# First sequence's chain, the mixer's beginning and the attention's last denominators: a change of order on one Trainium2 core

## The chip, the cores and the metric

The kernel runs on one core of one Trainium2 chip. The metric is the device time of one execution in microseconds (us), the median of several executions. The core has five engines with instruction queues of their own: PE (TensorE: matmuls and transposes, with its weight loads shown apart as PEld), DVE (VectorE), ACT (ScalarE: activation functions, whose tables are loaded by an instruction of its own), POOL (GpSimd) and SP (SyncE, which here issues the DMAs). Each runs its queue in order and waits at an instruction until the semaphores that it needs are set.

## The reference, cut to what matters

The input `x` is 8 sequences of 1024 tokens (32 × 32) with 128 channels, fp32. Two layers:

```python
x = x + attention(_gn(x))          # group norm, 4 heads of 32
t = _to_tokens(x)
t = t + mixer(_ln_t(t))            # two directions
t = t + spectral(_ln_t(t))         # filters by FFT, one of four banks chosen
```
Attention projects q, k and v, divides q and k by their lengths over the tokens, takes `softmax(10 * q k^T)` (in the kernel: Exp of the scores, their sums as denominators, reciprocals), multiplies with v and with `w_out`, and adds a bias. The mixer is, for each direction, an input projection, a causal convolution of four taps with SiLU, a step size `dt = softplus(x + bias)`, and a chunked state-space sum:

```python
Acs = jnp.cumsum(dAc, axis=2)
Lmat = jnp.exp(_segsum(dAc.transpose(0, 1, 3, 2)))
Y_diag = jnp.einsum('bcln,bcsn,bchls,bcshp->bclhp', Cc, Bc, Lmat, xc)
decay_st = jnp.exp(Acs[:, :, -1:, :] - Acs)
states = jnp.einsum('bcln,bclh,bclhp->bchpn', Bc, decay_st, xc)
new = st + carry * dec[:, :, None, None]     # from chunk to chunk
Y_off = jnp.einsum('bcln,bchpn,bclh->bclhp', Cc, prev, jnp.exp(Acs))
y = Y_diag + Y_off + xh * D
yn = rmsnorm(y * silu(z)) @ out_proj
```
Chunks are 64 tokens long, with 4 heads. The spectral stage needs, besides, tables of sines and a weight bank chosen by a softmax over four numbers.

## The kernel before, in words

The program is one launch in four stages: attention (0 to about 449 us), mixer (to about 1010), spectral stage with the filter matrices (to about 1370), and the end. Within attention the order of PE, DVE, ACT and POOL is the order of the program text; SP's is not fixed. Within the mixer all five are in the order of the text. So the Python text is the schedule: generators that `yield` are pieces of work that a loop picks up, one piece per slot.

**Start.** Sequence 0 is normalised and projected by the same generator as the others, `qkv` (L607), with `first` switching some steps: PE turns the tokens (`xt`, L612), ACT copies them, DVE takes statistics (L623), PE sums them over groups (`pm` L628, `pv` L636), POOL takes the root (`gn`), DVE scales (`xnt`, L641). PE projects `pq` and `pk` (L648); DVE copies each out of PSUM (L656), ACT squares each with a running sum (`junk`, L660), POOL makes the lengths (L665, L667), PE projects `pvl` (L671), DVE scales k (L684). Between these, lines 774–785 place the pieces of `transforms` (L311), which makes angle tables on POOL and DVE (`angles`, L282) for two trigonometric tables, `inv` and `fwd`, and for four lag tables; `sines` (L300) turns angles to sines on ACT.

**Attention.** 128 units: 8 sequences × 2 halves of queries × 8 key tiles. In slot n of the loop, `scores` (L692) issues unit n's matmuls (`pt`) and Exp (`pr`), `weigh` (L715) weighs v by unit n−1's (`po`), `total` (L738) sums denominators (`pd`) of two key tiles at a time. At the end of a half, `weighted` (L751) copies the denominators, takes four reciprocals in two pieces, the largest and the smallest of them (`most`, `least`), multiplies `av`, and `project` (L425) multiplies by `w_out` (`py`) and adds to X. The slots also take pieces of the next sequence's `qkv`, of `mixer_and_bank` (weights of the mixer, then `select_bank`, L205, then the mixing of the bank's matrices on POOL), of `transforms`, of the filters' taps, and, at the end, the first sequence's `dt` (`steps`, L480: bias, `sp_e` = Exp, `sp_u` = 1 + e, `sp_l` = Ln, `dt`, `da`).

**Mixer.** 16 units: 8 sequences × 2 directions (u.d 0 and 1). Lines 1253–1274 prepare the first unit by hand: `project_x` and `copy_x` for two halves (`pp`, `xp`), `add_decays` (L870: cumulative sums, `pdec`, copied to `cums` and `dsum` on ACT), what is left of `weighted` for the last half of attention with its projection `last_py`, `first_tap` (L970, ACT) and `convolve` (L976, DVE) for the taps, `turn_decays` (L885), `take_decays` (L891: Exp of `cums`, one store to DRAM and four loads that spread it over partitions, into `lm` and `ec`), `from_row` (L920, POOL, on `lm`), `project_bc` and `activate_bc` (`pb`, then `bt` and `ct`), and `compare_denominators` (L431: a test of the denominators' range, `far`, `pf`). `wide_psum(ps_w)` and `wide_psum(ps_s)` hand out slots of two PSUM pools.

The loop L1277–1352 then takes one unit `u` per turn and prepares the one `following`: `between` (L930, ACT, Relu then Exp on `lm`), `turn_x` (`sx`), `weigh_start` (POOL, `ec`), `turn_b` (`sb`, `bg`), the following unit's projections (`pp`), `weigh_decays`, the previous unit's `end` (L1239), `steps` for the next sequence where one is `fresh` (in turns with u.d = 0: 0, 2, …, 12), `project_z` and `activate_z` (`pz`, `zs`), `from_row(following)`, `chunk_states` and `pass_states` (`pst`, `state`, `moved`), the last tap, `project_bc`, and `outputs` in two halves (`sy`).

## Time and profile before

| | us |
|---|---|
| time, median of 3 executions (1420.01 to 1421.38) | 1420.11 |
| the profiled execution | 1414.25 |
| its span in the trace | 1412.4 |
| PE busy in it | 1325.0 |
| DVE busy | 1093.9 |
| ACT busy | 916.0 |
| POOL busy | 530.2 |
| mean granted TensorE clock, of full speed | 0.987 |

The profile is of one execution. A row of the timeline has its start from the span's beginning, its duration (of a run of like instructions together, with their number after x), the engine, the line, the operation, output and inputs by their names in the program, and, in brackets, how long the engine had been idle before it and what ended that idleness. A row of the waits has what waited, for what, the sum, the number and the longest. Matmuls are pipelined, and weight loads lie beside them. The busy share of a stage tells which engine bounds it, and only a wait on that engine, or at a place where it idles, costs time.

Times of the stages' ends that are used: attention's last product starts at 447.46, the mixer's first projection at 451.20, its first turn at 471.91 (`sx`), and the next turns' `sx` at 501.94, 534.37 and 569.40.

### The profile page before, as it was taken

How to read it: one execution, taken by the hardware profiler on the slowest of the kernel's cores; microseconds unless marked ns; L12 is line 12 of the kernel's file. 1: busy time of each engine (PE TensorE's matmuls, PEld its weight loads, DVE VectorE, ACT ScalarE, POOL GpSimd, SP SyncE). 2: the span in 40 equal slices, each digit the busy share in tenths (PEclk: the TensorE clock that was granted, in tenths of full speed). 3: DMA queues.
4: the chain of work that ended last, by engine and by line, in shares of the span. 5: the costliest groups of instructions: out<-in, count | busy, mean ns of one | idle time of the engine just before them, and what ended most of it. 6: DMA issues, size and time to landing. Idle time of an engine off the chain costs nothing. (4 is left out here: it accounts for less than half of the span.)

```text
span 1412.4 us, 45313 instructions
## 1 busy us (share of the span) xinstructions
PE 1325.0 (94%) x19798; PEld 836.2 (59%) x19798; DVE 1093.9 (77%) x2141; ACT 916.0 (65%) x1423; POOL 530.2 (38%) x510
## 2 busy tenths in 40 slices
PE   5999999999999899999999999998799899999977
PEld 2323333233333466666666666665689899999964
DVE  6789888787768698978897988889644677777745
ACT  3766666766757777878787878786454555555530
POOL 2426865875610333425243434343476111111100
PEclk9999999999999999999999999999999999999999
DMA  7101111110000543434344445441459233222257
GB/s 179 46 1 31 46 38 38 38 50 27 8 1 2 124 86 77 107 77 106 82 102 91 104 92 114 89 110 42 135 189 233 76 86 81 72 78 71 71 186 299
DMA packets 139382, 123.09 MB, mean 87 GB/s; under 512 B 44808, under 2 KB 118152, under 8 KB 135080
## 3 DMA queue, kind: packets, MB, share of 16 engines
q1 hardware_dynamic: 137048, 115.93, 32.1%
q10 hardware_dynamic: 2128, 4.19, 0.8%
q8 instruction: 157, 2.57, 0.8%
q14 instruction: 49, 0.40, 0.1%
HBM read 78.15 MB, written 34.08 MB: 79 GB/s over the span
## 5 line engine op out<-in xcount | busy, mean ns | idle before, releaser
L707 ACT ACTIVATE pr<-pt 128x1024 f32<-128x1024 f32 x256 | 248.1, 1021 | 114.9 <-PE pt L702 113.5
L732 DVE TENSOR_TENSOR two<-pr,pr 128x1024 f32<-128x1024 f32 x128 | 162.3, 1308 | 19.2 <-ACT pr L707 18.7
L1525 ACT COPY gs<-pg 128x512 f32<-128x512 f32 x256 | 132.4, 603 | 64.1 <-PE pg L1512 48.3
L1523 DVE COPY gs<-pg 128x512 f32<-128x512 f32 x256 | 158.7, 683 | 14.7 <-PE pg L1512 9.7
L702 PE MATMUL pt<-q,k 32*128 32x512 f32 x1024 | 157.6, 648 | 9.4 <-ACT pr L707 4.7
L1512 PE MATMUL pg<-taps,mst 32*128 32x128 f32 x4096 | 145.6, 281 | 4.2 <-ACT gs L1525 3.4
L1512 PEld LDWEIGHTS pg<-taps,mst 32*128 32x128 f32 x4096 | 133.8, 190 | 16.2 <-issue 11.4
L723 PE MATMUL po<-pr,v 128*32 128x512 f32 x1024 | 139.7, 603 | 0.0
L938 POOL TENSOR_TENSOR ec<-ec,ct 128x2048 f32<-128x2048 f32 x16 | 83.6, 5226 | 131.8 <-ACT cums L880 69.8
L1546 PE MATMUL py<-gs,u 128*32 128x128 f32 (+1 forms) x4096 | 128.5, 277 | 1.2 <-issue 1.2
L1002 PE MATMUL pb<-bxt,wbc 128*128 128x512 f32 x256 | 115.7, 605 | 11.0 <-ACT zs L993 11.0
L980 DVE SCALAR_TENSOR_TENSOR xs<-xp,cw,xs 128x1024 f32<-128x1024 f32 x96 | 121.7, 1281 | 1.7
L1546 PEld LDWEIGHTS py<-gs,u 128*32 128x32 f32 (+1 forms) x4096 | 112.4, 141 | 8.7 <-issue 1.5
L1535 POOL TENSOR_SCALAR u<-u 128x512 f32<-128x512 f32 x16 | 23.9, 1495 | 227.8 <-DMA u<-ud 114.0
L702 PEld LDWEIGHTS pt<-q,k 32*128 32x128 f32 x1024 | 46.6, 185 | 87.2 <-issue 33.1
L1002 PEld LDWEIGHTS pb<-bxt,wbc 128*128 128x128 f32 x256 | 47.7, 191 | 69.3 <-issue 54.9
L1099 DVE SCALAR_TENSOR_TENSOR state<-state,dec,pst 128x64 f32<-128x64 f32 x448 | 87.3, 274 | 1.5 <-DVE state L1096 0.5
L1208 POOL TENSOR_TENSOR rms<-rms_v,mhalf 128x8 f32<-128x8 f32 x16 | 27.1, 1696 | 159.7 <-DVE rms_v L1206 159.7
L723 PEld LDWEIGHTS po<-pr,v 128*32 128x32 f32 x1024 | 27.6, 110 | 88.3 <-issue 84.1
L924 POOL TENSOR_TENSOR lm<-cs,lm 128x2048 f32<-128x2048 f32 x16 | 57.9, 3620 | 46.9 <-DVE xs L980 31.4
L743 PE MATMUL pd<-two,ones 128*32 128x512 f32 x512 | 73.9, 612 | 0.2
L1178 PEld LDWEIGHTS spo<-wo,y 128*128 128x128 f32 x512 | 62.2, 192 | 15.3 <-issue 10.2
(288 smaller groups left out, 2757.7 us busy)
## 6 DMA issues: line engine op xcount, KB each, us to landing
lm<-cd SPq DMA_DIRECT2D x32, 512.0 KB
ec<-cd SPq DMA_DIRECT2D x32, 512.0 KB
ud<-sp SPq DMA_DIRECT2D x8, 1024.0 KB
u<-ud SPq DMA_DIRECT2D x32, 256.0 KB
yd<-sums SPq DMA_DIRECT2D x32, 256.0 KB
moved<-state SPq DMA_DIRECT2D x48, 128.0 KB
room<-yd SPq DMA_DIRECT2D x6, 1024.0 KB
X<-in_x SPq DMA_DIRECT2D x8, 512.0 KB
```

Source lines behind the costliest of these rows:

```text
L702: nc.tensor.matmul(pt[:, i, :], lhsT=k[rows, j * P : (j + 1) * P], rhs=q[rows, cols], start=True, stop=True)
L707: nc.scalar.activation(pr[:, 2 * g : 2 * g + 2, :].rearrange("p i t -> p (i t)"), pt.rearrange("p i t -> p (i t)"), AF.Exp, scale=SCALE,)
L723: nc.tensor.matmul(po[rows, :], lhsT=vs[b][:, j, rows], rhs=pr[:, h, :], start=(j == 0), stop=(j == NT - 1))
L732: nc.vector.tensor_tensor(two, sums["pr"][:, 2 * g : 2 * g + 2, :], pr[:, 2 * g : 2 * g + 2, :], ALU.add)
L938: t = nc.gpsimd.tensor_tensor(u.ec, u.ec, u.ct.unsqueeze(1).to_broadcast([P, NH, NT, L]), ALU.mult)
L980: u.convolved = nc.vector.scalar_tensor_tensor(acc, xp[:, at : at + T], cw[u.d][:, n, i : i + 1], acc, ALU.mult, ALU.add)
L1002: nc.tensor.matmul(u.pb[:, i * 512 : (i + 1) * 512], lhsT=wbc[u.d][:, k, :], rhs=xt[:, at : at + 512], start=(k == 0), stop=(k == KC - 1),)
L1099: nc.vector.scalar_tensor_tensor(u.state[:, k, h, :], u.state[:, k - 1, h, :], u.dec[:, c, h, j : j + 1], u.pst[c][:, j, h, :], ALU.mult, ...
L1512: nc.tensor.matmul(pts[g][:, e, :], lhsT=mst[rows, n * 4 + e, :], rhs=taps[rows, cols].rearrange("p f q m i -> p (f q m i)"), start=True, ...
L1523: nc.vector.tensor_copy(to, frm)
L1525: nc.scalar.copy(to, frm)
L1546: nc.tensor.matmul(py[t * 32 : t * 32 + 32 - 16 * m, q // 2, :], lhsT=u[:, i, m:, :, :, q * FC + f].rearrange("p k b i -> p (k b i)"), rhs ...
```

## The change

It has these parts:

- **First sequence**: a function of its own, `first_qkv`, takes the place of `qkv(0)`. DVE's statistics and ACT's copy take opposite halves of the turned tokens; 24 transposes whose result nobody reads (`busy`) are put on PE in three places; a Sin of one column (`soon`) loads the Sin table; the squares read PSUM; k is scaled out of PSUM; `fwd`'s and `inv`'s sines are taken there; the bias is added after k. `transforms` makes `fwd`'s angles first, then `inv`'s. The Sin of `fwd` leaves the later burst with the lag tables.
- **Bank choice**: three `yield`s in `select_bank` spread it over four slots.
- **`steps`**: a `yield` between `sp_u` and `sp_l`, with one more slot (n = 120) in attention, and one more pick-up in the mixer's loop, behind `activate_z` and `first_tap(following, 1)`.
- **Mixer's beginning**: in another order; `pdec` of the first unit and its `pb` are taken from the other PSUM pool; the rest of `weighted`, `last_py` and the comparison leave it.
- **Ending**: the rest of `weighted` is picked up in turns 0 (two pieces) and 1; the comparison and `last_py` are in turn 2, ahead of its second outputs.
- **Taps**: in turns with u.d = 0 all three DVE taps of the following unit's first half stand before the z projections; in turns with u.d = 1 two, as before.

```diff
@@ -219,6 +219,7 @@
         nc.scalar.activation(soft, logit, AF.Exp, bias=top, accum_out=total)
+        yield
         nc.vector.reciprocal(total, total)
@@ -228,9 +229,11 @@
         nc.vector.tensor_scalar(left, hard, -1.0, 1.0, ALU.mult, ALU.add)
+        yield
         for i in range(1, NM):
...
             nc.vector.tensor_tensor(left[:, i : i + 1], left[:, i : i + 1], left[:, i - 1 : i], ALU.mult)
+        yield
         w = pool.tile([P, NM], F32, name="w")
@@ -279,7 +282,7 @@
-    def angles(pool, dst, pieces, tag):
+    def turns(pieces):
@@ -287,7 +290,8 @@
                 nc.vector.tensor_scalar(to[:, :, i, :], numbers, by, turn, ALU.mult, ALU.add)
-        yield
+
+    def angles(pool, dst, tag):
@@ -310,28 +314,40 @@
+
+        def over_2048(t):
+            nc.vector.tensor_scalar(t, t, 1.0 / 2048.0, None, ALU.mult)
+
...
         place = counted(pool, [4], [[1, 4]], 0, 4, "place")
+        over_2048(place)
+        by_place = [(fwd[:, k : k + 1], odd[:, 0:1, :], place[:, k : k + 1]) for k in range(4)]
+        turns(by_place[:2])
+        yield
         odd_row = counted(pool, [1], [[1, 1]], 1, 2, "odd_row")
         places = counted(pool, [4, P], [[1, 4], [4, P]], 0, 0, "places")
+        over_2048(odd_row)
+        yield
+        turns(by_place[2:])
+        yield
+        for _ in angles(pool, fwd, "fwd"):
+            yield
+        yield
+        turns([(inv, places, odd_row[:, 0:1])])
+        for _ in angles(pool, inv, "inv"):
+            yield
         yield
         lag = counted(pool, [2, 2], [[-256, 2], [1, 2]], 510, -2, "lag")
-        for t in (place, odd_row, lag):
-            nc.vector.tensor_scalar(t, t, 1.0 / 2048.0, None, ALU.mult)
-        yield from angles(pool, inv, [(inv, places, odd_row[:, 0:1])], "inv")
-        yield
-        yield from angles(
-            pool, fwd, [(fwd[:, k : k + 1], odd[:, 0:1, :], place[:, k : k + 1]) for k in range(4)], "fwd"
-        )
-        yield
+        over_2048(lag)
         for h in range(2):
...
                 t = pool.tile([P, 2, 2, NF], F32, name=f"lags{h}_{r}")
-                for _ in angles(pool, t, [(t, odd, lag[:, h, r : r + 1])], f"lags{h}_{r}"):
+                turns([(t, odd, lag[:, h, r : r + 1])])
+                for _ in angles(pool, t, f"lags{h}_{r}"):
                     pass
...
                 yield
-        for t in (fwd, *tables):
+        for t in tables:
             sines(t)
@@ -510,6 +526,7 @@
         nc.vector.tensor_scalar(u, e, 1.0, None, ALU.add)
+        yield
         lg = small("sp_l")
@@ -611,16 +628,11 @@
-
-            first = b == 0
-            if first:
-                nc.scalar.copy(xt, pt)
-            else:
-                nc.vector.tensor_copy(xt, pt)
+            nc.vector.tensor_copy(xt, pt)
             yield
...
             for i in range(2):
-                nc.vector.bn_stats(st[:, i, :], (pt if first else xt)[:, i * 512 : (i + 1) * 512])
+                nc.vector.bn_stats(st[:, i, :], xt[:, i * 512 : (i + 1) * 512])
             mv = p2.tile([P, 2], F32, tag="mv", name=f"mv{b}")
@@ -657,10 +669,9 @@
                 junk = p1.tile([P, T], F32, tag="junk", name=f"junk{name}{b}")
-                nc.scalar.activation(junk, pq if first else to, AF.Square, accum_out=ss[:, i : i + 1])
+                nc.scalar.activation(junk, to, AF.Square, accum_out=ss[:, i : i + 1])
                 if i == 0:
-                    if not first:
-                        add_bias(xin)
+                    add_bias(xin)
                     yield
@@ -678,10 +689,90 @@
             vs.append(v)
-            if first:
-                add_bias(xin)
             yield
...
+
+        def first_qkv(making):
+
+            xin = X[0]
+            halves = [slice(0, 512), slice(512, T)]
+            next(making)
+            pt = ps_t.tile([P, T], F32, tag="t", name="xt0")
+            for j in range(NT):
+                nc.tensor.transpose(pt[:, j * P : (j + 1) * P], xin[:, j, :], ident)
+
+            busy = ps_o.tile([P, 512], F32, tag="d", name="busy")
+
+            def keep_busy(n):
+                for i in range(n):
+                    nc.tensor.transpose(busy[:, (i % 4) * P : (i % 4 + 1) * P], xin[:, i % NT, :], ident)
+
+            keep_busy(8)
+
+            soon = p2.tile([P, 1], F32, tag="soon", name="soon")
+            xt = p1.tile([P, T], F32, tag="xnt", name="xnt0")
+            st = p2.tile([P, 2, 6], F32, tag="st", name="st0")
+            for i in range(2):
+                nc.vector.bn_stats(st[:, i, :], pt[:, halves[i]])
+                nc.scalar.copy(xt[:, halves[1 - i]], pt[:, halves[1 - i]])
+            nc.scalar.activation(soon, mhalf, AF.Sin)
+            mv = p2.tile([P, 2], F32, tag="mv", name="mv0")
+            nc.vector.bn_aggr(mv, st.rearrange("p i s -> p (i s)"))
+            next(making)
+            pm = ps_t.tile([P, 1], F32, tag="t", name="pm0")
+            nc.tensor.matmul(pm, lhsT=group, rhs=mv[:, 0:1], start=True, stop=True)
+            keep_busy(4)
+            mean = p2.tile([P, 1], F32, tag="mean", name="mean0")
+            nc.vector.tensor_copy(mean, pm)
+            dm = p2.tile([P, 1], F32, tag="dm", name="dm0")
+            nc.vector.tensor_tensor(dm, mv[:, 0:1], mean, ALU.subtract)
+            nc.vector.scalar_tensor_tensor(dm, dm, dm, mv[:, 1:2], ALU.mult, ALU.add)
+            next(making)
+            pv = ps_t.tile([P, 1], F32, tag="t", name="pv0")
+            nc.tensor.matmul(pv, lhsT=group, rhs=dm, start=True, stop=True)
+            keep_busy(12)
+            var = p2.tile([P, 1], F32, tag="var", name="var0")
+            nc.vector.tensor_copy(var, pv)
+            rstd = rsqrt(p2, var, 1, 1.0, 1e-5, "gn")
+            next(making)
+            nc.vector.tensor_scalar(xt, xt, mean, rstd, ALU.subtract, ALU.mult)
+            next(making)
+            ss = p2.tile([P, 2], F32, tag="ss", name="ss0")
+            ps = []
+            for i, name in enumerate("qk"):
+                pq = ps_t.tile([P, T], F32, tag="t", name=f"p{name}0")
+                for cols in halves:
+                    nc.tensor.matmul(
+                        pq[:, cols], lhsT=wqkv[:, i * C : (i + 1) * C], rhs=xt[:, cols], start=True, stop=True
+                    )
+                junk = p1.tile([P, T], F32, tag="junk", name=f"junk{name}0")
+                nc.scalar.activation(junk, pq, AF.Square, accum_out=ss[:, i : i + 1])
+                ps.append(pq)
+            pvl = ps_t.tile([P, NT, P], F32, tag="t", name="pvl0")
+            for j in range(NT):
+                nc.tensor.matmul(
+                    pvl[:, j, :],
+                    lhsT=xt[:, j * P : (j + 1) * P],
+                    rhs=wqkv[:, 2 * C : 3 * C],
+                    start=True,
+                    stop=True,
+                )
+            nc.gpsimd.tensor_scalar(ss, ss, 1e-24, None, ALU.max)
+            lengths = p2.tile([P, 2], F32, tag="inv", name="inv0")
+            nc.gpsimd.tensor_tensor(lengths, ss, mhalf.to_broadcast([P, 2]), ALU.pow)
+            sines(fwd)
+            v = keepq.tile([P, NT, P], F32, tag="v", name="v0")
+            nc.scalar.copy(v.rearrange("p j d -> p (j d)"), pvl.rearrange("p j d -> p (j d)"))
+            vs.append(v)
+            next(making)
+            q, k = (keepq.tile([P, T], F32, tag=name, name=f"{name}0") for name in "qk")
+            nc.vector.tensor_copy(q, ps[0])
+            qs.append(q)
+            next(making)
+            sines(inv)
+            nc.vector.tensor_scalar(k, ps[1], lengths[:, 0:1], lengths[:, 1:2], ALU.mult, ALU.mult)
+            ks.append(k)
+            add_bias(xin)
@@ -768,19 +859,9 @@
         tables = []
-        going, making, coming = transform_taps(p1, ps_t, tables), transforms(p1, tables), qkv(0)
+        going, making, coming = transform_taps(p1, ps_t, tables), transforms(p1, tables), qkv(1)
         s.enter_context(tc.manual_schedule(engines=IN_ORDER))
-
-        next(making)
-        for at in range(10):
-            next(coming)
-            for _ in range({4: 3, 5: 1, 7: 1}.get(at, 0)):
-                next(making)
-            if at == 4:
-                sines(inv)
-        next(coming, None)
-        next(making)
-        coming = qkv(1)
+        first_qkv(making)
         next(coming)
@@ -823,7 +904,7 @@
                     next(sizes)
-            elif n in (121, 123):
+            elif n in (120, 121, 123):
                 next(sizes, None)
@@ -867,10 +948,10 @@
-        def add_decays(u):
+        def add_decays(u, pool=ps_w):
...
             u.dt, u.da = u.seq["dt"][:, :, u.heads], u.seq["da"][:, u.d]
-            ps = wide_psum(ps_w, f"pdec{u.tag}")
+            ps = wide_psum(pool, f"pdec{u.tag}")
             pd = ps[:, : 3 * NT * NH].rearrange("p (i h j) -> p i h j", i=3, h=NH)
@@ -992,10 +1073,10 @@
-        def project_bc(u):
+        def project_bc(u, pool=ps_w):
...
             xt = u.seq["xt"]
-            u.pb = wide_psum(ps_w, f"pb{u.tag}")
+            u.pb = wide_psum(pool, f"pb{u.tag}")
             for i in range(2):
@@ -1252,26 +1333,20 @@
         copy_x(first, 0)
-        add_decays(first)
-        for _ in ending:
-            pass
         first_tap(first, 0)
         project_x(first, 1)
+        add_decays(first, ps_s)
         copy_x(first, 1)
+        add_decays(units[1])
         turn_decays(first)
+        first_tap(first, 1)
         take_decays(first)
-        first_tap(first, 1)
-        convolve(first, 0, range(1))
-        project(B - 1, 1, av, wide_psum(ps_w, "last_py")[:, :512].rearrange("p (i c) -> p i c", i=4))
-        add_decays(units[1])
-        convolve(first, 0, range(1, pad))
-        activate_x(first, 0)
-        convolve(first, 1)
-        activate_x(first, 1)
+        project_bc(first, ps_s)
+        for n in range(2):
+            convolve(first, n)
+            activate_x(first, n)
         from_row(first, first.convolved)
-        project_bc(first)
         activate_bc(first)
-        compare_denominators(most, least, wide_psum(ps_w, "pf")[0:1, :2])
@@ -1302,6 +1377,8 @@
             weigh_decays(u, 0)
+            if at == 0:
+                next(ending)
             going = iter(())
@@ -1321,11 +1398,13 @@
             weigh_decays(u, 1)
-            convolve(following, 0, range(pad - 1))
+            soon = pad - u.d
+            convolve(following, 0, range(soon))
             for n in range(2):
...
             first_tap(following, 1)
+            next(going, None)
             for _ in normalized(b, bridge, *norm) if u.d else ():
@@ -1336,7 +1415,7 @@
             stored = None
-            convolve(following, 0, range(pad - 1, pad))
+            convolve(following, 0, range(soon, pad))
             activate_x(following, 0)
@@ -1344,6 +1423,13 @@
+
+            if at < 2:
+                next(ending)
+            elif at == 2:
+                room = wide_psum(ps_w, "last_py")
+                compare_denominators(most, least, room[0:1, 512:514])
+                project(B - 1, 1, av, room[:, :512].rearrange("p (i c) -> p i c", i=4))
             activate_x(following, 1)
```

## The prediction

> **What bounds the kernel now.** I read the busy times first, then the same busy times cut into stages, then PE's waits, and last the timeline around each edit.
>
> ```profile
> PE 1325.0 (94%) x19798; PEld 836.2 (59%) x19798; DVE 1093.9 (77%) x2141; ACT 916.0 (65%) x1423; POOL 530.2 (38%) x510
> 0.00:27.00 27.00, 12.44 (x48) 8.11 (x52) 15.85 (x34) 9.05 (x10) 9.48 (x32) 0.99 0.84 205
> 150.00:300.00 150.00, 147.02 (x1066) 48.62 (x1058) 126.03 (x147) 103.26 (x114) 109.39 (x99) 0.99 0.15 43
> 449.00:472.00 23.00, 18.83 (x71) 9.12 (x70) 16.67 (x24) 12.35 (x22) 5.94 (x13) 0.93 0.44 93
> 472.00:1010.00 538.00, 507.88 (x7910) 349.82 (x7911) 453.12 (x989) 418.56 (x660) 201.01 (x120) 1.00 0.40 90
> PE pb L1002 <- ACT zs L993: 11.0, 15, 1.3
> ```
> In the stage rows the columns after the length are PE, weight load, DVE, ACT and POOL busy, PE's clock, DMA share and GB/s. PE is full in attention (147 of 150) and the bound of the mixer (508 of 538). It idles for 14.6 us before the first scores and 4.2 us where the mixer starts. In the mixer its largest wait is on ACT's `zs`: 11 us in 15 places. So the change can win at the start, at that wait, and wherever attention is held by a burst on another engine.
>
> The start, in the timeline:
> ```profile
> 12.79 0.81 DVE L641 TENSOR_SCALAR xnt<-xnt,mean,gn 128x1024 f32<-128x1024 f32 x1 [0.97 <-POOL gn L132]
> 21.54 1.03 ACT L660 ACTIVATE junkk<-pk 128x1024 f32<-128x1024 f32 x1 [1.68 <-DVE k L656]
> 23.82 2.82 DVE L684 TENSOR_SCALAR k<-k,inv 128x1024 f32<-128x1024 f32 x1 [1.77 <-POOL inv L667]
> 26.78 2.09 PE L702 MATMUL pt<-q,k 32*128 32x512 f32 x8 [3.94 <-DVE k L684]
> 28.90 1.94 ACT L707 ACTIVATE pr<-pt 128x1024 f32<-128x1024 f32 x2 [4.04 <-PE pt L702]
> ```
> It is one chain: normalise, project, square, lengths, k, scores, Exp. k's square waited for DVE's copy of the same PSUM tile; the first Exp is at 28.90, the next pairs' at 31.81 and 34.95.
>
> The mixer's start, and a unit of a forward direction (unit 2):
> ```profile
> 466.89 3.62 POOL L924 TENSOR_TENSOR lm<-cs,lm 128x2048 f32<-128x2048 f32 x1 [13.21 <-DMA lm<-cd]
> 471.88 2.01 ACT L934 ACTIVATE lm<-lm 128x1024 f32<-128x1024 f32 x2
> 478.01 2.42 PE L947 MATMUL pp<-bxt,win 128*128 128x512 f32 x5 [0.59 <-ACT bg L1056]
> ```
> ```profile
> 553.00 1.28 ACT L514 ACT_TABLE_LOAD   x1
> 554.29 0.26 ACT L514 ACTIVATE sp_l<-sp_u 128x64 f32<-128x64 f32 x1
> 554.57 1.28 ACT L993 ACT_TABLE_LOAD   x1
> 555.86 1.94 ACT L993 ACTIVATE zs<-pz 128x1024 f32<-128x1024 f32 x2
> 556.94 7.13 PE L1002 MATMUL pb<-bxt,wbc 128*128 128x512 f32 x16 [1.20 <-ACT zs L993]
> ```
> Two table loads stand ahead of `zs`, and `pb` takes `zs`'s PSUM slot, so PE idles 1.20 us.
>
> [...] half clock from 26.20 to 33.02 after an idle stretch, two windows of 3.41. [...] from 1026.3 to 1029.7 half transposes, half matmuls ended a half-clock stretch. [...] Here the load is 1.28 us, and the next instruction starts 1.29 after it[...]. [...]
>
> **The change, part by part** (against the profiled 1414.25 us, span 1412.4; the median of the runs is 5.9 above it, so I carry the difference over).
>
> *A, the first sequence.* Now ACT's copy and bn_stats go half by half, each waiting for the other's half, and casts stand before `mean`: `xnt` is ready about 14.2 instead of 13.6 (+0.6). Twelve keep-busy transposes are queued ahead of pq: at half clock (242 ns each) they run 11.9 to 14.8. If they count, the clock is full from the boundary at 15.96 instead of 19.37 (multiples of 3.41). Then pq ends 16.9 (four matmuls, 0.85 before, 0.43 after), pk 18.6, k's square straight from PSUM 19.8, lengths on POOL +1.1 = 20.9, k from PSUM 1.22 = 22.1 (it took 2.82 beside POOL's bias add, now behind it), scores 1.0 = 23.2; the Exp load ends about 23.5 and v's copy and the moved Sin tables (1.06 each) fit before it. First Exp about 23.5, 5.4 earlier, and the second pair, no longer at half clock, 5.9 to 6.7 earlier. I take **−6.0**. If transposes do not count: pq 14.8 to 18.2, pk half-clocked to 19.4, first Exp about 26: −3.3. Bounds −2.5 and −7.
>
> *A2, the bank choice in four slots (n = 22, 24, 28, 30).* Before, some 20 DVE operations of 0.15–0.2 us and the small Exp stood in slot 22. Units 22–28 took 28.68 us, the same places a period later (38–44) 24.98: 3.7 lost, of it ACT's `soft`<-DVE `top` 2.9, which stays in slot 22 (about 1.2 net), and PE `py`<-DVE `av` 2.38, which is spread. **−2.0**, bounds −2.6 and −0.5. The mixing on POOL and the bank's SP loads move three slots later; POOL is 73% busy in 150–300 and no row there waits for it: 0, ending some 10 units later, still inside attention. One `sp_u` operation at n = 120: 0.2 us in DVE's idle: 0.
>
> *A3, one Sin (1.06) out of the burst at n = 73.* Units 73–76 took 19.53 against 14.87 in a quiet period and PE waited 2.98 for ACT's `pr` there: **−1.0** (−1.1, 0).
>
> *B, the mixer's beginning.* Four reciprocals (3.39), two reductions and a product (2.05), last_py (1.13) and the far comparison leave; pb moves ahead, into the other PSUM pool, 457.2 to 464.1. But PE's end here is not PE's own: `cums`' Exp → cd store (457.72) → loads of lm and ec (2 MB, 459.25 to about 468 at some 216 KB/us) → from_row 466.89 to 470.5 → relu 471.88 → load, Exp of lm → `bg` copy → `pp` at 478.01. take_decays is now behind the second add_decays and the second first_tap (1.24): its Exp at about 458.7 instead of 457.35, so lm lands +1.35, from_row ends about 471.9. Before, relu was held by ct (to 471.2), 1.4 behind from_row; so relu starts about 471.9 again: **0**, bounds −3 (sx, sb and bg free of lm's chain) and +1.4.
>
> *C, units with a fresh sequence (0, 2, …, 12).* Ln moves behind both `zs` and first_tap(1). `zs` then starts after one load, at 554.29, its first half ends 555.26, before the states' matmuls end (555.75): the wait 1.195, 1.197, 1.194, 1.290, 1.193, 1.189 of units 2–12 goes (unit 0 has 0.2): 6 × 1.2 = **−7.2**. Added: a third load on ACT, 1.28 × 7, and the third tap, 1.28 on DVE, ahead of from_row. Their cover: DVE idles 2.11 before the states (553.67–555.78). from_row starts 555.05 instead of 553.80, relu ends 560.8, the Silu load 562.1; `xs` formerly waited until 563.77 for DVE's last tap, which is now done before. So xs ends 563.2 against pb's end 562.9, and bt, ct, sx follow 1.2 earlier. The states' second transfers feed only the second outputs. ACT is 26.8 busy of 35.0, DVE 28.4. Bounds −8 and, if that cover fails, the third rival.
>
> *D, the ending inside units 0–2.* Unit 0: two reciprocals (1.75) ahead of `sp_v` and hence of pz (which waited 0.31 for it): +0.4; two more in DVE's 2.5 idle: 0. Unit 1: 3 × 0.68 = 2.05 ahead of xdt in 2.05 idle: +0.3. Unit 2: PE's far product and last_py (0.2 + 1.13) stand between pdec and the second outputs; PE waits for DVE's reductions, and all that PE does next is queued behind it: +2.3. **+3.0**, bounds +1 and +5. Before, this work lay in the shadow of the lm chain.
>
> Sum: −6.0 − 2.0 − 1.0 + 0 − 7.2 + 3.0 = **−13.2**: profiled about 1401.0, median 1420.1 − 13.2 = 1406.9.
>
> **Rivals.**
> 1. *Cold clock*: [...]transposes don't count; A is −3.3: 1409.6. [...]Against: 1026–1029. Within it the transposes only delay pq by 0.6.
> 2. *The beginning gains too*: the sx–sb–bg stretch does not hang on lm, or fewer colliding loads let it land sooner; B −4: 1402.9. For: PE idles 4.2 there. Against: the chain above.
> 3. *Slower*: in the seven fresh units the extra load with Ln (1.54) and the tap (1.28) end up on from_row → relu → Silu load → xs → bt, ct → next sx. This decides once that chain runs over 1.5 us later than I computed (bt formerly 564.74, now 563.2). At the full 2.8 it costs 7 × 2.8 = +19.7 and C's gain is gone: 1420.1 − 9 + 19.7 + 3 = 1433.8. For: ACT runs in order, and relu and xs stand behind. Against: the 2.96 that xs waited for DVE.
> 4. *It doesn't do what it says in attention*: the small operations stall elsewhere (A2 and A3 0), D costs 5 and C gives half: −6 − 3.6 + 5 = −4.6: 1415.5; with the cold clock as well −1.9, within 0.2%.
>
> **Chances.** Forecast 0.55, rival 1 0.15, rival 2 0.10, rival 4 0.13 (a third of it within 0.2%), rival 3 0.07. About 0.2% (2.8 us) is what a measurement of this kernel can tell from no change. The forecast's own range, A to D at their bounds, about halved as they are independent, is ±4. With rivals 1 and 2, and half of 4, the range is 1400 to 1414. Faster 0.88, same 0.05, slower 0.07.
>
> **What would show it.** A: first Exp near 23.5, pk's matmuls 0.43 each (warm) or 0.85 (cold). A2: no `py`<-`av` wait of 2 us near unit 24. B: `pp` of unit 1 still 6.1 us after sx, from_row waiting for lm. C: the row `pb`<-`zs` down from 11.0 to about 4, fresh units about 33.8 instead of 35.0. D: unit 2 longer by 1, and a wait on `far`. I am wrong if fresh units stay at 35 or more with `sx` waiting for ACT's `xs`, or if the units 0 to 2 lose more than 5.

## The result, and the profile after

Over 20 executions of each kernel the median is 1418.53 us (1413.84 to 1426.13) against 1419.73 us for the kernel before: a ratio of 0.9997, with a 95% interval of 0.9983 to 1.001 (the medians alone would give 0.9992). Nothing changed that can be measured, where 13.2 us had been forecast. The profiled execution took 1416.98 us (span 1415.3). That of the kernel before, 1414.25 us, was the shortest of all that were measured of that kernel (the next 1415.19); a second profile of it, below, took 1420.47.

The page and the waits of the changed kernel:
```profile
PE 1337.4 (94%) x19822; PEld 845.3 (60%) x19822; DVE 1100.7 (78%) x2140; ACT 924.8 (65%) x1432; POOL 532.2 (38%) x510
```
```profile
PE sb L1129 <- DVE xdt L1115: 10.1, 15, 3.9
...
PE pp L1028 <- ACT bg L1137: 6.5, 1, 6.5
...
PE pb L1083 <- ACT zs L1074: 3.6, 8, 0.5
...
PE last_py L454 <- DVE far L453: 0.9, 1, 0.9
```
PE is 12.4 us busier for 24 added transposes (8.6 against the second profile of the kernel before): much of the same work took longer. The wait of `pb` for `zs` fell from 11.0 to 3.6, as forecast, but `bg` (0.6 before) and `xdt` (7.1 before, never over 0.4 at a time) now hold PE. Stages of the changed kernel (length, then PE, weight load, DVE, ACT and POOL busy, PE's granted clock, DMA share, GB/s): turn 0 up to `pp`, the rest of turn 0, and turn 2.
```profile
459.00:472.40 13.40, 5.60 (x90) 4.65 (x89) 2.45 (x2) 9.25 (x16) 8.26 (x6) 0.95 0.54 114
472.40:500.60 28.20, 27.83 (x369) 16.16 (x369) 23.51 (x52) 19.80 (x23) 5.30 (x2) 0.84 0.43 93
532.20:574.60 42.40, 37.40 (x518) 27.11 (x518) 35.48 (x67) 27.99 (x42) 13.00 (x10) 0.92 0.30 64
```
Turns 0 and 2 of the kernel before:
```profile
471.90:501.90 30.00, 28.45 (x457) 18.95 (x457) 22.42 (x50) 23.63 (x31) 8.70 (x7) 1.00 0.41 89
534.30:569.40 35.10, 33.38 (x508) 23.19 (x508) 28.44 (x58) 26.82 (x41) 10.55 (x8) 1.00 0.35 77
```
Up to `pp`, turn 0 has PE busy for 5.6 of 13.4 us; then the mean clock is 0.84 in the rest of turn 0 and 0.92 in turn 2, where before it was 1.00. The granted clock takes two values in these two traces, 1.0 and 0.5 of full speed (the matmuls of `pb` in the first profile of the kernel before followed each other by 0.43 us at the first and by 0.85 at the second), and "half clock" below is a stretch of the second. Milestones of the two profiles, changed minus before:

| | us |
|---|---|
| first Exp / third unit's Exp | −5.2 / −3.8 |
| behind the bank choice (unit 30) / unit 48 / end of attention | −7.3 / −4.6 / −5.1 |
| turn 0's sx / turn 1's sx | −12.5 / −1.3 |
| turn 2's sx / turn 3's sx | −2.1 / +5.3 |
| last turn's sx | −0.1 |

So the gains are there, turn 0 gives back 11.2 us and turn 2 7.4, and the turns behind it win 5.3 again.

The start of the changed kernel:
```profile
13.27 0.81 DVE L738 TENSOR_SCALAR xnt<-xnt,mean,gn 128x1024 f32<-128x1024 f32 x1 [0.74 <-POOL gn L132]
...
14.19 1.96 PE L745 MATMUL pq<-xnt,wqkv 128*128 128x512 f32 x4
...
21.06 1.34 DVE L773 TENSOR_SCALAR k<-pk,inv 128x1024 f32<-128x1024 f32 x1 [0.60 <-POOL inv L762]
...
22.55 4.32 PE L793 MATMUL pt<-q,k 32*128 32x512 f32 x16 [2.04 <-DVE k L773]
...
23.72 2.85 ACT L798 ACTIVATE pr<-pt 128x1024 f32<-128x1024 f32 x3 [0.54 <-PE pt L793]
```
The first Exp is within 0.3 us of the forecast (the clock was up before `pq`, at 13.68). Then the clock falls to half from 23.92 to 30.75, and the second unit takes 5.58 us instead of 3.14. Turn 0 and turn 2:
```profile
462.67 3.62 POOL L1005 TENSOR_TENSOR lm<-cs,lm 128x2048 f32<-128x2048 f32 x1 [14.11 <-DMA lm<-cd]
...
466.32 2.00 ACT L1015 ACTIVATE lm<-lm 128x1024 f32<-128x1024 f32 x2 [4.03 <-POOL lm L1005]
...
472.45 6.39 PE L1028 MATMUL pp<-bxt,win 128*128 128x512 f32 x8 [6.53 <-ACT bg L1137]
```
```profile
531.53 4.22 DVE L854 TENSOR_TENSOR av<-av,den 128x512 f32<-128x512 f32 x1
...
530.64 4.56 POOL L1019 TENSOR_TENSOR ec<-ec,ct 128x2048 f32<-128x2048 f32 x1 [7.32 <-ACT cums L961]
...
538.07 1.15 PE L1129 MATMUL sb<-ident,bt 64*64 64x64 f32 x32 [3.85 <-DVE xdt L1115]
...
540.67 1.97 PE L489 MATMUL px<-ident,ln_x 128*128 128x128 f32 x8
...
569.82 1.89 PE L443 MATMUL last_py<-wout,av 128*128 128x128 f32 x8 [0.24 <-DVE far L455]
```
`pp` follows the `lm` chain where it was forecast (478.01 − 5.6), but its eight matmuls take 6.39 us instead of 3.71: PE had idled 6.5 us, and the clock was at half from 471.06 to 477.89. The product with av takes 4.22 us instead of 0.68 and ends 0.6 us behind the POOL instruction beside it; PE then waits 3.85 for xdt and turns the tokens (`px`) at half clock (1.97 instead of 1.09).

### The profile page after: what moved, and what is told of

It reads as the page before. It is cut to its first block, busy times and chain, and to the rows that moved or that the text cites. A ratio compares the mean times of both kernels' runs of the same rounds, so it can differ in the third digit from the quotient of the medians.

```text
span 1415.3 us, 45362 instructions
## 1 busy us (share of the span) xinstructions
PE 1337.4 (94%) x19822; PEld 845.3 (60%) x19822; DVE 1100.7 (78%) x2140; ACT 924.8 (65%) x1432; POOL 532.2 (38%) x510
```

## The experiments

Theory: the ending inside turns 0 to 2 lost its cover and costs two things that my sum did not hold, a stall of a DVE instruction beside a POOL one (4.22 us instead of 0.68), and half clock behind idle stretches of PE (`pp` 6.39 us instead of 3.71 behind 6.5 idle). Rivals: the losses are half-clock stretches that would fall anyway; or the forecast gains are not there. A ratio below is to the kernel before, with its 95% interval, and "us" is its distance from 1, times 1420. Where two edited kernels are compared, ± is their two intervals taken together.

**The ending back in the mixer's beginning.**
```diff
         copy_x(first, 0)
+        for _ in ending:
+            pass
...
         activate_bc(first)
+        room = wide_psum(ps_w, "last_py")
+        compare_denominators(most, least, room[0:1, 512:514])
+        project(B - 1, 1, av, room[:, :512].rearrange("p (i c) -> p i c", i=4))
...
-            if at < 2:
-                next(ending)
```


> The changed kernel with the ending back in the mixer's beginning: the four reciprocals, the largest, the smallest and the product with av behind the first copy of x, the comparison and last_py ahead of the first turn; nothing else. Theory (the ending inside turns 0 to 2 ate the gains): turn 2 falls from 42.4 to about 33.8 us, and DVE's work lies in the time in which it waits for ACT and for lm; 9 to 11 us faster than the changed kernel, so about 1409 against 1419.7 of before. Rival (the clock's half windows, wherever they fall, set the difference, not the ending's place): within 3 us of the changed kernel.

0.9944 (0.9922 to 0.9966): −8.0 us against before, and 7.5 ± 3.7 us faster than the changed kernel, somewhat less than the expected 9 to 11. Turn 2 takes 33.9 us, turn 0 35.0 instead of 41.2. The rival's 3 us is just excluded.

**The product with av away from POOL.**
```diff
-            if at == 0:
+            if at in (0, 2):
                 next(ending)
             going = iter(())
...
-            if at < 2:
+            if at == 0:
                 next(ending)
```


> The changed kernel with one edit: the third piece of the ending (most, least, product with av) is picked up in turn 2 behind the first weighing of decays, where DVE idles about 3 us and POOL is idle, instead of at the end of turn 1 beside POOL's product on ec. Theory (the product's 4.22 us is a stall behind the POOL instruction that runs beside it, and PE's wait of 3.9 for xdt with the half-clock window behind it is its consequence): the product takes 0.68, the wait falls to 0.44, and turn 2 from 42.4 to about 37; 4 to 6 us faster than the changed kernel. Rival (the product is slow for what stands before it on DVE, or PE's clock falls for another reason): the product stays over 2 us, or turn 2 over 41.

0.9976 (0.9961 to 0.999): −3.4 us against before, 3.0 ± 2.8 faster than the changed kernel, where 4 to 6 had been expected. In its timeline the product is short and sb no longer waits:
```profile
544.49 0.68 DVE L854 TENSOR_TENSOR av<-av,den 128x512 f32<-128x512 f32 x1
...
533.40 1.15 PE L1129 MATMUL sb<-ident,bt 64*64 64x64 f32 x32 [0.45 <-DVE xdt L1115]
```
Turn 2 falls to 36.2. So the stall, 4.22 us against 0.68, hangs on the POOL instruction beside it. The turn is 6 us shorter; how this divides between the stall and the clock shows after the next run.

**PE kept busy where it waits for bg; and in the start.**
```diff
+            if at == 0:
+                busy = wide_psum(ps_s, "busy_mixer")
+                for i in range(48):
+                    nc.tensor.transpose(busy[:, (i % 8) * P : (i % 8 + 1) * P], X[0][:, i % NT, :], ident)
             between(u, AF.Exp, -1.0, (1,))
```


> The changed kernel with 48 transposes whose result nobody reads on PE in turn 0, behind the turned tokens and ahead of the following unit's projection, where PE idles 6.5 us for bg. Theory (the idle stretch takes the clock away, and the next projections run at half clock): pp stays at 0.43 a matmul, turn 0 falls from 41.2 to about 37.5, some 3 to 4 us faster than the changed kernel. Rival (the clock doesn't matter there, since ACT and DVE set the pace of turn 0): turn 0 stays within 1 us, and so does the time.

0.9972 (0.9962 to 0.9982): −4.0 us against before, 3.5 ± 2.4 faster than the changed kernel. Turn 0 takes 37.2, at full clock throughout:
```profile
470.96 3.71 PE L1028 MATMUL pp<-bxt,win 128*128 128x512 f32 x8 [1.70 <-ACT bg L1137]
```
```profile
457.50:494.70 37.20, 33.88 (x507) 24.23 (x506) 25.46 (x54) 28.07 (x38) 12.97 (x8) 1.00 0.53 112
```
Work of no use made the kernel faster. In this profile turn 2 too ran at full clock, though the stall was in it (the product took 4.21 us). Turn 2 of the run with the product apart, then of this one:
```profile
530.99:567.22 36.23, 34.55 (x519) 24.20 (x518) 31.91 (x68) 28.10 (x42) 13.10 (x8) 1.00 0.35 75
```
```profile
527.29:566.28 38.99, 34.55 (x519) 24.20 (x518) 34.02 (x67) 28.11 (x42) 11.69 (x8) 1.00 0.32 70
```
So turn 2 comes apart:

| turn 2 | us | mean clock |
|---|---|---|
| the ending back in the beginning | 33.9 | 1.00 |
| comparison, `last_py` and product in it, the product apart from POOL | 36.2 | 1.00 |
| the product beside POOL: this run, and the one without transposes below | 39.0, 39.2 | 1.00 |
| the same: changed kernel, and the next run | 42.4, 43.2 | 0.92, 0.88 |

The work itself costs 2.3 us, the stall 2.8 to 3.0 more, and half clock, where it fell into the turn, another 3 to 4.

The other fill, ahead of the first scores:
```diff
         next(coming)
+        busy = ps_o.tile([P, 512], F32, tag="d", name="busy_scores")
+        for i in range(14):
+            nc.tensor.transpose(busy[:, (i % 4) * P : (i % 4 + 1) * P], X[1][:, i % NT, :], ident)
         next(coming)
```

> The changed kernel with 14 transposes whose result nobody reads between the second sequence's turned tokens and the first scores, where PE idles 2 us. Theory (this idle stretch ends the full clock at 23.9 us, which costs the second and third units what the first gained): the clock stays full past 24, the third unit's Exp comes near 29 us instead of 31.1, 2 us faster than the changed kernel. Rival (PE idles behind the first scores as well, so the clock falls one window later anyway): the half-clock stretch only moves, and the gain is under 0.7 us.

0.9992 (0.9979 to 1.0005): not told from none, nor from the changed kernel. Its third unit's Exp was at 28.5 (−6.5 against before), with no half clock there; but the run with the ending back, which has no such transposes, had none there either. Of the ten profiles with the new start, its 24 transposes and no such fill, five have half clock between 22 and 33 us and five have none. What decides between them is not shown.

**One part alone, on the kernel before.** The hunks are those of the change. The fresh turns:
```diff
+        yield
         lg = small("sp_l")
...
-            convolve(following, 0, range(pad - 1))
+            soon = pad - u.d
+            convolve(following, 0, range(soon))
...
             first_tap(following, 1)
+            next(going, None)
```

> The kernel before with one part of the change: Ln behind both zs and the second first tap (with its pick-ups in attention's slots and in the mixer), and all three taps ahead of the z projections in forward turns. Theory (this part gives what was forecast): the wait of pb for zs falls from 11.0 to about 4, the fresh turns 2 to 12 go from about 35.1 to 33.9 us, the kernel 7 us faster than before (ratio 0.995). Rival (the freed PE time is taken back at the next place in the turn): fresh turns over 34.6, under 3 us in all.

0.9936 (0.9921 to 0.9951): −9.1. Turns 2, 4 and 6 take 34.0 to 34.1 us instead of 35.0 to 35.1, and `pb`'s wait in them is gone, as expected.

The ending:
```diff
-        for _ in ending:
-            pass
...
+            if at < 2:
+                next(ending)
+            elif at == 2:
+                room = wide_psum(ps_w, "last_py")
```


> The kernel before with the ending alone moved: the four reciprocals, most, least, the product, the comparison and last_py go from the mixer's beginning to turns 0, 1 and 2 as in the change; the beginning's order is otherwise that of before. Theory (the moved work was hidden and is not hidden any more, and it brings a stall[...] and half-clock windows): the third turn's length rises from 35.0 to 42 or more, the sum of turns 0 to 2 by 7 to 10 us, some of it given back where the beginning has less to do; 5 to 9 us slower than before. Rival (the ending costs 3 us, as forecast, and the rest was lost elsewhere): 1 to 3 us slower.

1.0057 (1.0043 to 1.0071): +8.1 us. Turn 2 takes 43.3 us instead of 35.0, with the same 4.22 us beside POOL and a mean clock of 0.92; up to turn 2 nothing is lost (turn 2 starts 84.9 us behind attention's end, before 85.2). The whole loss of this part is in turn 2:
```profile
536.80 4.22 DVE L763 TENSOR_TENSOR av<-av,den 128x512 f32<-128x512 f32 x1
```
The first sequence:
```diff
+        first_qkv(making)
         next(coming)
```


> The kernel before with the first sequence's part alone (its own chain, the order of the tables, one Sin less in the later burst). Theory (the start gives about two thirds of what was forecast, for the clock falls to half at the wait behind the second sequence's transposes in some executions): third Exp 4 to 6 us earlier than before, one more behind slot 73, in all 4 to 6 us faster. Rival (the start's gain is lost at the next collision in attention): under 2 us.

0.9946 (0.9925 to 0.9966): −7.7. The third unit's Exp came 6.3 us earlier.

**No keep-busy transposes.** This one leaves out the 24 transposes; the output does not depend on them.
```diff
-            keep_busy(8)
...
-            keep_busy(4)
...
-            keep_busy(12)
```

> The changed kernel without the 24 transposes in the first sequence. Theory (transposes count for the clock): the projections of q, k run at 0.85 a matmul at least in part, the clock comes up one or two windows later, near 19, and the first Exp at 25 to 26.5 instead of 23.7 to 24.9. Rival (they don't count, and the clock came up for the matmuls and the turned tokens): first Exp as before or earlier.

```profile
14.18 3.75 PE L735 MATMUL pq<-xnt,wqkv 128*128 128x512 f32 x4 [2.53 <-issue]
```
`pq` took 3.75 us instead of 1.96, the clock came up at 19.82 instead of 13.68, and the first Exp at 26.0: the transposes counted. Plainer still is `pm`, the first product behind the turned tokens. In the profile of the first sequence alone PE had run nothing but transposes (from 5.05 us on) when the full clock came at 8.07, and `pm` ran at it; without the added transposes it ran at half:
```profile
9.46 0.35 PE L719 MATMUL pm<-mv,group 128*128 128x1 f32 x2 [1.01 <-DVE odd_row L309]
```
```profile
9.46 0.56 PE L715 MATMUL pm<-mv,group 128*128 128x1 f32 x2 [2.48 <-DVE odd_row L312]
```
As a whole this run took 0.9971 (0.9956 to 0.9987): 3.7 ± 2.9 us faster than with the transposes. So with them the clock was up 6.1 us earlier, but no gain in time from them is shown, and what the new start is worth is not shown to rest on them. Why the kernel without them should be the faster one stays open.

**The kernel before again**, for a second profile.

> The kernel before, unchanged, for a second profile. The first profiled execution was 5.9 us below the median of its runs. Theory (that execution happened to be short, in the stages behind the mixer): the mixer ends at about the same place (its last sx within 2 us of 972.4) and what follows takes 443 to 447 us instead of 440. Rival (it is the changed kernels that are slower behind the mixer): 440 again.

Both figures missed by a little: the last `sx` came 3.7 us later than in the first profile, and what follows took 442.4 us instead of 440.0. The first profile was of a short execution. Part of the rest stays with the rival: in the changed kernel and the 15 with other edits this stretch took 442.8 to 447.8.

**Where the rest was.** The parts did not yet sum to the result, so the reordered beginning and the bank choice were run alone, and two parts together.

```diff
-        add_decays(first)
...
+        add_decays(first, ps_s)
         copy_x(first, 1)
+        add_decays(units[1])
...
+        project_bc(first, ps_s)
```


> The kernel before with the mixer's beginning in the changed order, but with the ending kept in it (its reciprocals, most, least and product behind the first copy of x, the comparison and last_py ahead of the first turn). Theory (the reordering itself costs: it issues the store of the decays about 1.3 us later, and PE, done earlier, waits and loses its clock): the second unit's pp starts 0 to 2 us later than before relative to the end of attention, a half-clock window more near 480, 2 to 5 us slower than before. Rival (it is neutral, as forecast): within 1.5 us of before.

1.0023 (1.001 to 1.0036): +3.3. PE idles 3.46 us in front of `pp`, and the clock is at half behind it (0.9 us a matmul; in the fastest run, below, eight took 3.71):
```profile
481.58 3.62 PE L947 MATMUL pp<-bxt,win 128*128 128x512 f32 x4 [3.46 <-ACT bg L1056]
```
The chain is not neutral either, though the first profile makes it seem so. `pb` of the first unit in the first profile of the kernel before; `pb` and the first Relu on `lm` in its second profile; the Relu in this run:
```profile
459.60 8.81 PE L1002 MATMUL pb<-bxt,wbc 128*128 128x512 f32 x16
```
```profile
461.80 7.12 PE L1002 MATMUL pb<-bxt,wbc 128*128 128x512 f32 x16
...
472.39 2.00 ACT L934 ACTIVATE lm<-lm 128x1024 f32<-128x1024 f32 x2
```
```profile
475.45 2.00 ACT L934 ACTIVATE lm<-lm 128x1024 f32<-128x1024 f32 x2 [2.72 <-POOL lm L924]
```
In the first profile, and in no other, half clock (459.69 to 463.10) stretched `pb`, and `ct` behind it held the Relu: it came 20.7 us behind the start of the first projection. In the second profile, and in five runs that keep that beginning, it came after 19.0 to 19.3; in this run after 20.5, and in six others with the new order after 20.2 to 20.8. So issuing the store later costs 1 to 1.8 us, and the half clock comes on top.

The bank choice, with the change's three `yield`s:

> The kernel before with the bank choice alone spread over four slots. Theory (3.5 us are gained in slots 22 to 28, and 2 to 3 are given back in slots 33 and 43, where the shifted work on POOL makes the bias addition stand ahead of DVE's sum): 0 to 1.5 us faster than before. Rival (the shift costs more later): slower.

0.9994 (0.9981 to 1.0007): −0.9. Units 22 to 30 gain 3.5 us, units 33 and 43 lose 2.7. In unit 43, with POOL's work three slots later, the bias addition comes first and DVE's sum waits behind it (two took 4.50 us instead of 2.88):
```profile
163.30 2.52 POOL L608 TENSOR_TENSOR X<-X,bout 128x1024 f32<-128x1024 f32 x1
163.54 4.50 DVE L735 TENSOR_TENSOR two<-pr,pr 128x1024 f32<-128x1024 f32 x2
```
The first sequence and the fresh turns together, each as above:

> The kernel before with the first sequence's part and the part of the fresh turns (Ln, taps), without the other parts. Theory (the two gains are in different stages and add): 7.7 + 8.3 = 16 us faster, ratio 0.989. Rival (each was partly the luck of the clock's windows): 10 to 12 us faster.

0.9929 (0.9909 to 0.9949): −10.1, not −16.8. The rival's size holds: the two gains, in different stages, don't add in full. Its reason, luck with the clock, isn't shown. In the profile, of the longest of its six executions, turns 2, 4 and 6 took 33.7 to 34.0 us, so the fresh turns' gain was there; but half clock lay at 12.1 to 18.9 and at 25.8 to 32.6, the third unit's Exp came only 1.9 us earlier than before instead of 6.3, and what follows the last `sx` took 447.8 us.

**Towards a faster one.** With the ending back, first `bg`'s copy ahead of the Relu; then, instead, the decays taken at once, directly behind the first projection (the second first_tap also moves up a place):
```diff
             if at == 0:
+                turn_x(u)
+                turn_b(u)
+                turn_tokens(fresh, seqs[fresh], wide_psum(ps_w, f"px{fresh}"))
                 between(u, AF.Relu, 1.0)
```

> The changed kernel with the ending back in the mixer's beginning (as in the earlier run), and in turn 0 the turned x, B and tokens, with their copies out of PSUM, ahead of the first Relu on lm, so that bg's copy does not stand behind what waits for lm. Theory (PE's wait at turn 0 is ACT's order: bg's copy stands behind the Relu that waits for lm's loads): pp no longer waits for bg, turn 0 shrinks by 3 to 5 us against the earlier run, the kernel gains as much: about 1408. Rival (lm is needed right behind, by the weighed decays, so the wait only moves to pz or to sy): under 1.5 us.

0.993 (0.9912 to 0.9948), not told from the run with the ending back (2.0 ± 4.0 us faster; 3 to 5 expected). `pp` starts at 466.1, but the next product waits 4.4 us for the copies of `pp`, which stand behind the same Relu and Exp; turn 0 takes 38.1. The wait only moved.

```diff
         project_x(first, 0)
+        add_decays(first, ps_s)
+        take_decays(first)
         copy_x(first, 0)
```


> The changed kernel with the ending back in the mixer's beginning, and the first unit's decays taken at once: add_decays and take_decays (Exp of cums, the store and the loads of lm and ec) directly behind the first projection, ahead of the copies and of the second unit's decays. Theory (the beginning hangs on the chain store, loads, from_row, Relu, Exp, bg): the store is issued 3 to 4 us earlier and pp of the second unit starts 2 to 3.5 us earlier than with the ending alone put back; about 1409. Rival (the loads collide with nothing and from_row waits for the taps behind which it stands): under 1 us.

0.9887 (0.9867 to 0.9907): −16.0 against before, the fastest, and 8.1 ± 4.2 us faster than the run with the ending back, its like but for the early decays. The profiles show less of it: the store is issued 3.9 us behind the start of the first projection instead of 7.9, the Relu and turn 1 come 1.9 us earlier behind attention's end (2 to 3.5 expected). Where the rest came from isn't shown. PE hardly waits:
```profile
472.93 3.71 PE L1028 MATMUL pp<-bxt,win 128*128 128x512 f32 x8 [0.55 <-ACT bg L1137]
```
```diff
-            if n in (9, 25, 41, 57, 73):
+            if n in (9, 25, 45, 57, 73):
...
+                for i in range(24):
```


> The kernel of the run before this one, with 24 transposes whose result nobody reads where PE waits for bg in turn 0, and with the lag table of slot 41 made in slot 45 instead. Theory: no half-clock window near 470, turn 0 shorter by 1 to 3 us; and the sum of two probabilities that stood 2.1 us behind the bias addition on POOL in slot 43 no longer does, 2 us of attention: some 3 us faster than the run before. Rival (the transposes delay pp, the collision moves to another slot): within 1 us of it.

0.994 (0.9919 to 0.9961): 7.5 ± 4.1 us slower than the run before, where 3 us faster had been expected, though its own profile was 1.7 us shorter. Unit 43 fell to 2.9 us, but unit 47 took 7.1, PE waiting 3.1 for DVE's sum, which now stood behind the lag table. That offsets the gain; why the other executions were slower stays open.

```diff
-        yield
         nc.vector.reciprocal(total, total)
```
(and the other two `yield`s of the bank choice)

> The kernel of the earlier run with the decays taken at once, with the bank choice in one slot as before. Theory (spreading the bank choice nets nothing): within 2 us of that run's 0.9887. Rival (the spread was worth its 3.5 us, or cost): off by more.

0.9912 (0.9891 to 0.9934): 3.5 ± 4.2 us slower than with the spread. That is off by more than the theory's 2 us, but not told from none.

## Why the prediction was wrong

| part | forecast | alone, measured (95%) |
|---|---|---|
| first sequence and the Sin (A, A3) | −7.0 | −7.7 (−10.7 to −4.8) |
| bank choice (A2) | −2.0 | −0.9 (−2.7 to +1.0) |
| beginning's order (B) | 0 | +3.3 (+1.4 to +5.1) |
| fresh turns (C) | −7.2 | −9.1 (−11.2 to −7.0) |
| ending (D) | +3.0 | +8.1 (+6.1 to +10.1) |

With A and C taken together (−10.1), the parts sum to −10.1 − 0.9 + 3.3 + 8.1 = +0.4; the change measures −0.4. Against the forecast, D is off by 5.1 us, B by 3.3, A2 by 1.1, and A with C by 4.1.

- **The step that failed most is D, "+3.0, bounds +1 and +5": it cost 8.1.** The places were right (`sp_v` in turn 0, the second outputs in turn 2), and so was "+2.3" for the work in turn 2 (36.2 against 33.9). "Unit 1: 3 × 0.68 = 2.05 ahead of xdt in 2.05 idle: +0.3" was not: it took 0.68 from a row where POOL did nothing, and beside POOL's product on `ec` the third took 4.22, which lengthened turn 2 by 2.8 to 3.0. And the sum has no term for the clock, which added 3 to 4 in turn 2 where it fell to half (`last_py` then took 1.89 instead of 1.13).
- **B, "0", failed too: it cost 3.3.** The steps of the chain were read rightly, but from one execution. That the 1.35 us of later loads would hide behind `ct` held only there, since half clock had stretched `pb` from 7.12 to 8.81; everywhere else they are lost. That `pp` started where it was put in the changed kernel's profile is this coincidence. And I took PE's idle time there as free, but half clock followed it: `pp` 6.39 instead of 3.71. Transposes in that gap shortened turn 0 by 4.0 us. Before, PE waited only 0.6 us there.
- **A** held in size, and the chain was shortened as read; A3's units 73–76 took 18.58 us instead of 19.53. What the transposes add is in part luck: `pq` took between 1.96 and 3.75 us in the eleven kernels that have them, the first Exp came at 23.7 to 25.8, and the price of a pause behind the tokens (2.04 us of idle PE, half clock at 23.92) was missed. The third unit's Exp lay 1.9 to 6.5 us ahead of before. Rival 1, the cold clock, fell as a reading of the trace; in the time its 2.7 us cannot be seen, for the kernel without transposes was not slower.
- **A2** gained its units 22–28 (3.5), but "0" for POOL's shift was wrong: 2.7 came back in units 33 and 43, in 43 as a DVE sum that waited beside POOL.
- **C** held: 1.25 and 1.35 us in turns 4 and 6, with the third table load and tap under their cover. Turn 10 is an exception in that profile (35.2 us, no gain; 33.7 with this part alone).
- Rival 4 named D at 5 and came nearest, for part of the right reason; none of the rivals held half clock as a price of waiting.

Both stalled DVE instructions end a little behind the POOL instruction beside them: the product of 4.22 us 0.6 behind it, the two sums of 4.50 us 2.2 behind. That is about what they take where POOL does nothing (0.68; two sums 2.36, at 447.31 in the kernel before). Why DVE is held there is not shown. The forecast didn't ask what POOL does beside a moved DVE instruction.

Open: why A and C give 10.1 together and 16.8 apart, a difference of 6.7 with an interval of about ±4.5. That both move the half-clock stretches in what follows is a guess of mine, not shown. So 4.1 us of the miss have no shown cause.

## What to carry to other kernels

Before moving work out of a wait, price the wait twice: what is hidden in it, and what PE's clock loses when PE stands still (here `pp` took 6.39 us instead of 3.71 behind 6.5 us of idle PE). For each moved DVE instruction look up what POOL runs beside its new place; a duration from the old place is not the one at the new (here 0.68 and 4.22). A wait that hides something in one profile may be that execution's own (here `pb`, 8.81 in one and 7.12 in the next), so take a second profile before building on it. And when a beginning hangs on one chain of transfers, start that chain early (turn 1 came 1.9 us sooner) rather than clearing the engine that waits for it and starting the chain later (+3.3).

## What the runs showed of the hardware

- Transposes alone brought TensorE's full clock in these runs. In the profile of the first sequence alone it came at 8.07 us after 3 us of nothing but transposes; in the eleven profiles with the 24 added ones it first came between 8.07 and 16.74 us (13.68 in the changed kernel), in the seven without them between 16.87 and 19.82 (19.37 in the first profile of the kernel before, 19.82 in the changed kernel without them). It did not always last: in two of the eleven it had gone again before `pq`, which took 3.75 us.
- In the profile of the changed kernel and the first of the kernel before, half clock came in stretches of 3.41, 6.83 and 10.24 us (but for the one that the program's end cuts apart). They lie in part at other places in the two profiles of the kernel before (26.20 to 33.03 and 459.69 to 463.10 in the first, 23.70 to 33.94 and 484.50 to 487.91 in the second). Time went with them: of the 20 executions of the changed kernel, the shortest (1413.84 us) had the highest mean clock, 0.986, and the longest (1426.13) the lowest, 0.977. The last `sx` of one kernel lay 3.7 us apart in two profiles, so a milestone of one profile is no surer than that.
